# Splitting six seven-fold products a second time in a two-layer fp32 cross-attention kernel

## The chip, the cores and the metric

The kernel runs on one core of a Trainium2 chip. Its time is the device time of one execution in microseconds (us). Three runs before the change took 641.01, 641.02 and 641.52 us; the median is 641.02. Profiled executions are timed too, and their traces are read here.

The core has five engines with queues of their own. TensorE (PE in the profile) multiplies matrices into PSUM; its weight loads are listed apart, as PEld. VectorE (DVE) adds, reduces and transposes 32x32 blocks. ScalarE (ACT) applies functions and copies. GpSimd (POOL) does slow element-wise work and issues transfers. SyncE (SP) issues most transfers. Each engine takes its instructions strictly in order and waits on semaphores for the others.

## The reference

Two layers work on x (8 batches, 100 rows, 1024 columns) and a context c (8 batches, 1444 rows, 512 columns), all in fp32:

```python
# layer 0
Q = x @ Wq + bq; K = c @ Wk + bk; V = c @ Wv + bv
x = x + softmax(Q @ K.T / 32, axis=-1) @ V @ Wo + bo
# layer 1
q = x @ Wq + bq; k = c @ Wk + bk; v = c @ Wv + bv
w = softmax(q @ k.T / 32, axis=1)          # over the 100 rows of x
y = w @ v + x
out = (y - mean(y)) / sqrt(var(y) + 1e-6) * gamma + beta
```

## The kernel before

The kernel never forms K or V. It multiplies weights first: `wqk0` = Wq Wk^T (1024 x 512) and `wvo` = Wv Wo (512 x 1024) for layer 0, and `wqk1` for layer 1. The `queries` are x times wqk (transposed, 512 x 800), and scores are queries times the raw context. What the biases bq, bk and bv contribute are weighted sums over rows of the weights. `accumulate` (L305) forms them on VectorE with one `tensor_scalar` and seven `scalar_tensor_tensor`. `block_sums` (L355) transposes and reduces such a row, and `totals` (L363) finishes it with a small matmul.

**Stages.** In order: qk0 (`weight_products`, L241), vo0 (the same function), queries of layer 0 (L416), qk1, then softmax rounds for layer 0. In round b, `alternated` (L824) weaves the weighted rows of batch b with the scores of batch b+2 on TensorE. Then come `project0` for layer 0's output (L643), queries of layer 1, the rounds and projections of layer 1, and the normalised output.

**Seven-fold products.** Each weight product and each queries stage splits its matrices into 2 x 2 blocks (A11 to A22, B11 to B22) and forms the result from seven block products instead of eight, with sums S1, S2 and so on of the A blocks and T1, T2 and so on of the B blocks. The sums are made by `combine` (L165) on VectorE, often in place over a block that is no longer needed. A block product is `half_product` (L151). It is a run of matmuls over four chunks of 128 rows, accumulated into a pair of PSUM banks. The profile names the banks: qk_x, qk_z, qk_y, qk_w for the weight products of layers 0 and 1, vo_x and so on for vo0, g_x and so on for the queries. `put` copies a finished bank pair to the result with ScalarE, and `add` adds one on VectorE. x and y each hold several products in turn. There are six banks of one pool for x, z and y and two of another for w.

A first-level product in qk0 and qk1 is 16 matmuls of 256 columns, in vo0 eight of 512, in a queries stage eight of 400.

**Buffers.** The weights and the context stream through ten buffers (`unit`), loaded by SyncE (L252 to L267, L499, L510). A load waits until the last reader of its buffer is done. Other pools are small: `row` has 3 buffers, `wide` 2, `gT` 3, and `weight_rows` (the transposed softmax rows) 3. The three `prob` tiles hold scores.

**Order.** TensorE runs in the order of the program. The other engines are ordered by the Tile framework's planner, from the dependencies and from its own estimates of durations, except where the code pins an instruction. `keep_in_program_order` pins it behind the instruction that was traced just before it on its engine. `vector.in_order` (L89) does so for all VectorE instructions issued through `vector`.

Of the kernel before, what the change touches and what calls it, by code (L numbers as in the profile page):

```python
# [25 lines left out]
F32 = mybir.dt.float32  # L26
AF = mybir.ActivationFunctionType
ALU = mybir.AluOpType
# [3 lines left out]
P = 128  # L32
# [23 lines left out]
def two_layer_cross_attention(ctx: ExitStack, tc: tile.TileContext, a: dict, out: bass.AP):  # L56
# [77 lines left out]
    for t in prob:  # L134
        nc.gpsimd.memset(t[T // QD * QD :, :], 0.0)
        nc.gpsimd.memset(t[:, S:], 0.0)
# [14 lines left out]
    def half_product(banks, lhs, rhs, fresh, nb, width):  # L151

        per = nb // len(banks)
        for i in range(len(lhs)):
            for n in range(nb):
                nc.tensor.matmul(  # L156
                    banks[n // per][:, n % per * width : (n % per + 1) * width],
                    lhs[i][:, n * P : (n + 1) * P],
                    rhs[i],
                    start=(fresh and i == 0 and n % per == 0),  # L160
                    stop=(i == len(lhs) - 1),
                    skip_group_check=True,
                )

# [74 lines left out]


    def weight_products(name, left, right, l_width, r_width, scaled):  # L241
# [10 lines left out]
        if name == "qk0":  # L252
            for part in (slice(0, lh // 2), slice(lh // 2, lh)):
                nc.scalar.dma_start(out=units[0][:, part], in_=lsrc[:, 0, part])
            nc.sync.dma_start(out=units[0][:, l_width : l_width + rh], in_=rsrc[:, 0, :rh])
            for h in range(1, EC):
                nc.sync.dma_start(out=units[h][:, :lh], in_=lsrc[:, h, :lh])
                nc.sync.dma_start(out=units[h][:, l_width : l_width + r_width], in_=rsrc[:, h, :])
                if h == 1:
                    nc.sync.dma_start(out=units[0][:, l_width + rh : l_width + r_width], in_=rsrc[:, 0, rh:])  # L260
            for i in range(H):
                for h in (i, H + i):
                    nc.sync.dma_start(out=units[h][:, lh:l_width], in_=lsrc[:, h, lh:])
        else:
            for h in range(EC):
                nc.sync.dma_start(out=units[h][:, :l_width], in_=lsrc[:, h, :])
                nc.sync.dma_start(out=units[h][:, l_width : l_width + r_width], in_=rsrc[:, h, :])  # L267

# [29 lines left out]
        def add(r, c, banks):  # L298
            for j in range(2):
                to = block(r, c, j)  # L300
                nc.vector.tensor_tensor(to, to, banks[j].rearrange("p (n w) -> p n w", n=per), ALU.add)

        accs = {}

        def accumulate(side):  # L305
            for v, of in scaled:
                if of != side:
                    continue
                width = (l_width, r_width)[side]
                if width == E:  # L310
                    acc = row(f"{name}_{v}")
                else:
                    acc = work.tile([P, L], F32, tag="half", name=f"{name}_{v}", bufs=1)
                accs[v] = acc
                for h in range(EC):
                    src = units[h][:, :l_width] if side == 0 else units[h][:, l_width : l_width + r_width]
                    if h == 0:
                        nc.vector.tensor_scalar(acc, src, cols[v][:, h : h + 1], None, ALU.mult)
                    else:
                        nc.vector.scalar_tensor_tensor(acc, src, cols[v][:, h : h + 1], acc, ALU.mult, ALU.add)  # L320
# [5 lines left out]
        combine(S1, A21, A22, ALU.add)  # L326
        Z = pair("z")
        product(Z, A12, B21, True)
        accumulate(1)
        add(0, 0, Z)  # L330
# [3 lines left out]
        combine(B11, B22, T1, ALU.subtract)  # L334
        T2 = B11
        combine(B21, B21, T2, ALU.subtract)
        W = pair("w")
        product(W, A22, B21, True)
        put(1, 0, W)
        combine(S1, S1, A11, ALU.subtract)  # L340
        S2 = S1
        combine(B12, B22, B12, ALU.subtract)
        product(X, S2, T2, False)
        put(0, 1, X)
        accumulate(0)
        combine(A21, A11, A21, ALU.subtract)
        combine(A12, A12, S2, ALU.subtract)
        product(X, A21, B12, False)
        add(1, 0, X)
        add(1, 1, X)  # L350
        product(Y, A12, B22, False)
        add(0, 1, Y)
        return dst, [accs[v] for v, _ in scaled]

    def block_sums(name, t, sums):  # L355

        nc.vector.transpose(t, t)  # L360
        nc.vector.tensor_reduce(sums, t.rearrange("p (c q i) -> p c q i", q=P // QD, i=QD), AX.X, ALU.add)
# [42 lines left out]
    def key_biases(name, kb, bqbk):  # L404

        sums = quarter_sums(name)[:, :B, :]
        t = row(f"{name}_t").rearrange("p (b q j) -> p b q j", q=P // QD, j=QD)
        for g in range(B // G):

            src = bass.AP(kb[g].tensor, kb[g].offset, [list(kb[g].ap[0]), [T, G], [QD, P // QD], [1, QD]])  # L410
            nc.vector.transpose(t[:, g * G : (g + 1) * G], src)
        nc.vector.tensor_reduce(sums, t, AX.X, ALU.add)
        c = totals(name, sums, B)
        nc.vector.tensor_scalar(c, c, SCALE, bqbk, ALU.mult, ALU.add)
        return c

    def queries(layer, w, u):

        H = EC // 2

        def half(g):
            return xT[:, :, g * GT : (g + 1) * GT]

        cols = [slice(j * 256, j * 256 + 256) for j in range(2)]
        A11, A12, A21, A22 = ([w[:, k * H + i, c] for i in range(H)] for c in cols for k in range(2))
        Bs = [[half(g)[:, k * H + i, :] for i in range(H)] for g in range(2) for k in range(2)]
        S1, S2 = (chunks(row(f"g{layer}_s{n}").rearrange("p (c l) -> p c l", c=H), H) for n in (1, 2))
        T1, T2 = (chunks(wide(f"g{layer}_t{n}"), H) for n in (1, 2))
        T3 = chunks(work.tile([P, LC, GT], F32, tag="gT", name=f"g{layer}_t3", bufs=3), H)
        dst = [work.tile([P, LC, GT], F32, tag="gT", name=f"g{layer}T_{g}", bufs=3) for g in range(2)]  # L430
        A, S, T_ = (A11, A12, A21, A22), (S1, S2, A21, A12), (T1, T2, T3, T1)
# [6 lines left out]
        def add(r, g, banks):  # L438
            for j in range(2):
                to = dst[g][:, 2 * r + j, :]  # L440
                nc.vector.tensor_tensor(to, to, banks[j][:, :GT], ALU.add)

        steps = seven_products(
            f"g{layer}",
            A,
            Bs,
            S,
            T_,
            2,
            GT,  # L450
            put,
            add,
            lambda n: left_sums(A, S, (n,)),
            lambda n: right_sums(Bs, T_, (n,)),
        )
        return dst, steps


    wqk0, (acc_c, acc_u) = weight_products(
# [3 lines left out]
    for g in range(B // G):  # L463
# [5 lines left out]
    wvo, (acc_o,) = weight_products("vo0", "L0_xattn_WvT", "L0_xattn_Wo", L, E, (("L0_xattn_bv", 1),))  # L469
    sums_u = quarter_sums("u0")[:, :LC, :]  # L470
    block_sums("u0", acc_u, sums_u)
    sums_c = quarter_sums("c0")
    block_sums("wqbk0", acc_c, sums_c[:, :EC, :])
    gT = [None, None]
    gT[0], steps = queries(0, wqk0, totals("u0", sums_u, LC))
    run(steps)
    block_sums("bvo", acc_o, sums_c[:, EC:, :])
    got = totals("wqbk0", sums_c, 2 * EC)
    wqbk0 = got[:, :EC]
    nc.vector.tensor_tensor(out_bias, out_bias, got[:, EC:], ALU.add)  # L480
    kb0 = [key_bias_sums(f"kb0_{g}", g * GT, (g + 1) * GT, wqbk0) for g in range(B // G)]
    wqk1, (acc_c, acc_u) = weight_products(
        "qk1", "L1_xattn_WqT", "L1_xattn_WkT", E, L, (("L1_xattn_bk", 0), ("L1_xattn_bq", 1))
    )
    c0 = key_biases("c0", kb0, bqbk0)
    for e in range(EC):
        nc.gpsimd.tensor_scalar(xT[:, e, :], xT[:, e, :], out_bias[:, e : e + 1], None, ALU.add)  # L487
    sums = quarter_sums("k1")
    block_sums("u1", acc_u, sums[:, :LC, :])
    block_sums("wqbk1", acc_c, sums[:, LC : LC + EC, :])  # L490
    got = totals("k1", sums[:, : LC + EC, :], LC + EC)
    u1, wqbk1 = got[:, :LC], got[:, LC:]
# [349 lines left out]
    for b in range(B):  # L842
        if b == B - 1:

            o0 = list(project0(AS, A0))
            next(o0[0])
            next(o0[0])
        run(alternated(b, 0, softmax0, A0[b // G][:, :, b % G * T : (b % G + 1) * T]))
        if b == 1:
            AS = value_sums(wvo)  # L850
    next(o0[1])
# [4 lines left out]
    for n in range(6):  # L856
        next(steps)
        if n == 0:
            kb1 = [key_bias_sums(f"kb1_{g}", g * GT, (g + 1) * GT, wqbk1) for g in range(B // G)]
    key_bias[1] = key_biases("c1", kb1, bqbk1)  # L860
# [59 lines left out]
```

## Time and profile before

| what | value |
|---|---|
| median of three runs | 641.02 us |
| profiled execution, its own time | 642.15 us |
| its span, first to last instruction | 640.3 us |
| TensorE busy | 628.8 us (98%) |
| VectorE busy | 457.0 us (71%) |
| ScalarE busy | 132.1 us (21%) |
| GpSimd busy | 101.8 us (16%) |
| moved by transfers | 127.28 MB |

Part 2 of the page divides the span into 40 slices of 16 us, and each digit is the busy share in tenths. The chain that ended last goes back from the last instruction to whatever released it. A line of it reads: start, duration in us, engine, what it writes, line of the program, count. The list of waits reads: who waited for whom, total us, times, longest. TensorE's ends are modelled, since matmuls overlap. The starts of consecutive instructions tell its pace. The same holds for VectorE, where an instruction's duration overlaps a little with the next.

### The profile page before, as it was taken

The numbers are of one execution on the slowest core, as the hardware profiler recorded it, in microseconds if no ns is written. First come the engines' busy times: TensorE is split into PE (matmuls) and PEld (weight loads), VectorE is DVE, ScalarE is ACT, GpSimd is POOL, SyncE is SP. The second block draws the span as 40 slices with busy tenths as digits, with TensorE's granted clock in tenths as the row PEclk, the third lists the DMA queues.
The fourth block names the chain that finished last, engine by engine and source line by source line (L and its number), as shares of the span: only waits on it lengthen the run. The fifth ranks groups of instructions, "written<-read, shape, count | busy, mean of one in ns | idle before, by whom it ended". The sixth has DMA issues, their size and how long they took to land.

```text
span 640.3 us, 9944 instructions
## 1 busy us (share of the span) xinstructions
PE 628.8 (98%) x3968; PEld 518.0 (81%) x3968; DVE 457.0 (71%) x864; ACT 132.1 (21%) x337; POOL 101.8 (16%) x118
## 2 busy tenths in 40 slices
PE   8999999999999999999999999999999999999994
PEld 7886445568885999999998655556999999999992
DVE  5999959569823775666655798229786659898886
ACT  1010010100103333212330000123332340325301
POOL 5000000009200000000010000007212220454054
PEclk9999999999999999999999999999999999999998
DMA  9928019000079799899896303046788990599002
GB/s 290 384 86 333 0 49 340 0 1 0 2 268 364 264 320 302 306 314 323 300 336 214 126 1 131 2 156 212 265 308 306 310 321 35 193 329 333 28 20 83
DMA packets 47907, 127.28 MB, mean 199 GB/s; under 512 B 3890, under 2 KB 6450, under 8 KB 47862
## 3 DMA queue, kind: packets, MB, share of 16 engines
q1 hardware_dynamic: 45784, 120.85, 54.6%
q0 software_dynamic: 1680, 5.33, 2.4%
q8 instruction: 31, 0.51, 0.3%
q10 hardware_dynamic: 398, 0.47, 0.2%
q14 instruction: 14, 0.11, 0.1%
HBM read 123.36 MB, written 3.28 MB: 198 GB/s over the span
## 4 chain that ended last, share of the span: by engine, by line
PE 94%; DVE 2%; issue 1%; DMA 1%; POOL 1%; POOLq 0%; SPq 0%; ACT 0%; DVEq 0%
PE s L560 25%; PE A L531 24%; PE qk_x L156 5%; PE g_x L156 5%; PE o_x L156 5%; PE qk_y L156 4%; PE g_y L156 3%; PE vo_x L156 3%; PE o_y L156 3%; PE qk_w L156 2%; PE vo_y L156 2%; PE g_w L156 2%; PE g_z L156 2%; PE o_w L156 2%; PE o_z L156 2%; PE qk_z L156 1%
## 5 line engine op out<-in xcount | busy, mean ns | idle before, releaser
L531 PE MATMUL A<-w,c 120*128 120x100 f32 (+1 forms) x1536 | 247.5, 265 | 0.0
L531 PEld LDWEIGHTS A<-w,c 120*128 120x128 f32 (+1 forms) x1536 | 215.9, 190 | 0.8
L93 DVE STREAM_TRANSPOSE w<-prob 32x384 f32<-32x384 f32 (+1 forms) x256 | 143.7, 561 | 37.3 <-ACT prob L572 15.1
L560 PE MATMUL s<-cT,g1T 128*100 128x131 f32 (+2 forms) x592 | 122.8, 297 | 0.0
L560 PE MATMUL s<-cT,g0T 128*100 128x131 f32 (+2 forms) x592 | 122.7, 296 | 0.0
L560 PEld LDWEIGHTS s<-cT,g1T 128*100 128x100 f32 x592 | 78.3, 167 | 8.9 <-ACT g1T L436 0.9
L560 PEld LDWEIGHTS s<-cT,g0T 128*100 128x100 f32 x592 | 78.3, 167 | 8.3
L572 ACT ACTIVATE prob<-s,c 100x393 f32<-100x393 f32 (+2 forms) x64 | 35.1, 560 | 116.7 <-PE s L560 116.4
L682 ACT ACTIVATE w<-w,negmax 120x100 f32<-120x100 f32 (+1 forms) x96 | 34.8, 364 | 82.3 <-DVE negmax L93 82.3
L487 POOL TENSOR_SCALAR xT<-xT,L_xattn_bo 128x800 f32<-128x800 f32 x8 | 20.8, 2609 | 134.0 <-PE qk_x L156 134.0
L592 DVE TENSOR_REDUCE maxima<-prob 100x1 f32<-100x394 f32 (+3 forms) x32 | 16.6, 528 | 28.1 <-ACT prob L572 27.9
L156 PE MATMUL qk_x<-qk 128*128 128x256 f32 x128 | 29.0, 382 | 1.0 <-DMA qk<-in_L_xattn_WkT 1.0
L701 POOL TENSOR_TENSOR part<-w 120x500 f32<-120x500 f32 x8 | 10.9, 1365 | 112.9 <-DVE rstd L776 28.6
L156 PEld LDWEIGHTS qk_x<-qk 128*128 128x128 f32 x128 | 23.7, 190 | 5.3 <-DMA qk<-in_L_xattn_WqT 1.3
L865 POOL DMA_DIRECT2D vectors<-in_L_xattn_gamma x1 | 0.6, 604 | 163.2 <-DMA c<-in_ctx 163.2
L320 DVE SCALAR_TENSOR_TENSOR qk_L_xattn_bk<-qk,L_xattn_bk,qk_L_xattn_bk 128x1024 f32<-128x1024 f32 x14 | 17.9, 1277 | 3.3 <-DMA qk<-in_L_xattn_WqT 3.2
L436 ACT ACTIVATE g1T<-g_x,k 128x400 f32<-128x400 f32 x6 | 3.6, 594 | 74.2 <-PE g_x L156 63.8
L93 DVE TENSOR_TENSOR xT<-xT,o_x 128x400 f32<-128x400 f32 (+1 forms) x32 | 15.9, 540 | 3.9 <-PE o_x L156 3.7
L682 ACT ACTIVATION_READ_ACCUMULATOR w<-w,negmax 120x1 f32 (+1 forms) x96 | 17.9, 187 | 0.0
L781 POOL TENSOR_TENSOR z<-z,vectors 100x1024 f32<-100x1024 f32 x7 | 16.5, 2352 | 8.2 <-ACT z L780 8.2
L759 PE MATMUL z<-ident,xT 128*100 128x128 f32 x64 | 16.3, 273 | 0.0
L93 DVE TENSOR_TENSOR w<-w,rtotal 120x400 f32<-120x400 f32 (+1 forms) x24 | 15.6, 649 | 0.7
(212 smaller groups left out, 869.4 us busy)
## 6 DMA issues: line engine op xcount, KB each, us to landing
cT<-in_ctxT SPq DMA_DIRECT2D x64, 722.0 KB, 6.6
c<-in_ctx SPq DMA_DIRECT2D x48, 768.0 KB, 8.5
c<-in_ctx SPq DMA_DIRECT2D x16, 512.0 KB, 6.8
vo<-in_L_xattn_Wo SPq DMA_DIRECT2D x8, 512.0 KB, 5.4
qk<-in_L_xattn_WqT SPq DMA_DIRECT2D x8, 512.0 KB
qk<-in_L_xattn_WqT SPq DMA_DIRECT2D x15, 256.0 KB, 5.4
qk<-in_L_xattn_WkT SPq DMA_DIRECT2D x15, 256.0 KB, 6.3
c<-in_ctx SPq DMA_DIRECT2D x16, 224.0 KB, 6.5
```

Of the source, the lines that this page charges most:

```text
L93: ins = getattr(nc.vector, op)(*args, **kw)
L156: nc.tensor.matmul(banks[n // per][:, n % per * width : (n % per + 1) * width], lhs[i][:, n * P : (n + 1) * P], rhs[i], start=(fresh and i ...
L320: nc.vector.scalar_tensor_tensor(acc, src, cols[v][:, h : h + 1], acc, ALU.mult, ALU.add)
L487: nc.gpsimd.tensor_scalar(xT[:, e, :], xT[:, e, :], out_bias[:, e : e + 1], None, ALU.add)
L531: nc.tensor.matmul(ps[:, k * T : (k + 1) * T], c[m // CQ][:r, m % CQ, k * P : (k + 1) * P], w[:r, m, :], start=(m == 0 and k == 0), stop=( ...
L560: nc.tensor.matmul(banks[n // per][:T, cuts[n] - o : cuts[n + 1] - o], q[:, k, t0 : t0 + T], cT[k][:, cuts[n] : cuts[n + 1]], start=(k == ...
L572: nc.scalar.activation(p[:, part], ps[:T, : part.stop - part.start], AF.Identity, bias=key_bias[layer][:T, b : b + 1], scale=SCALE,)
L592: nc.vector.tensor_reduce(maxima[:, n : n + 1], p[:, part], AX.X, ALU.max)
L682: nc.scalar.activation(w[:r, m0 + m, :], w[:r, m0 + m, :], AF.Exp, bias=negmax[:r, m : m + 1], accum_out=total[:r, m : m + 1])
L701: add(part, w[:MR, 0:5, :], w[:MR, 5:10, :], ALU.add)
L759: nc.tensor.transpose(ps[:T, e * P : (e + 1) * P], xT[:, 4 * j + e, b * T : (b + 1) * T], ident)
L781: nc.gpsimd.tensor_tensor(z, z, beta[:T], ALU.add)
```

## The change

Six of the first-level products are themselves formed from seven half-size products. They are w and the last one of vo0, the same two of qk1, and w of each of the two queries stages. The new function is `inner_product`. It makes four sums when it is called and the other four between its products. Its seven products of w are woven with the matmuls of the product v (A21 by B12, into x's banks). The last product of vo0 and qk1 becomes the inner product `Q`, run on its own after v; its parts are added to the result one by one.

From the third first-level product on, VectorE's instructions of vo0, qk1 and the queries are pinned in the order of the program. The queries' sums are one wide instruction each instead of four.

In qk0 the second product's successor is now w instead of y, with new buffers t2 and t4 for its sums, and its loads come in another order: the left and right first halves, then the right second halves, then the left second halves.

The bias sums of full width in vo0 and qk1 are made by `transferred_sum`. ScalarE scales eight rows into eight buffers (2 `row`, 3 `weight_rows`, 3 `prob`), and transfers issued by GpSimd, which add to their destination, sum them in three levels. qk1's narrow bias sum moves ahead of its products, into the queries stage. Block sums, key-bias sums, the addition of the output bias to x (now on ScalarE, two chunks a round in rounds 0 to 3), the memsets of `prob`'s last rows and layer 0's `value_sums` move to other places.

```diff
     for t in prob:
-        nc.gpsimd.memset(t[T // QD * QD :, :], 0.0)
         nc.gpsimd.memset(t[:, S:], 0.0)
...
+    def inner_product(name, lhs, rhs, nb, width, t, put, add):
+        h, w = nb // 2, width // 2
...
+        combine(S1, A21, A22, ALU.add)
+        combine(T1, B12, B11, ALU.subtract)
+        combine(A21, A11, A21, ALU.subtract)
+        combine(B12, B22, B12, ALU.subtract)
...
+        def steps():
+            X = bank(f"{name}_x")
+            product(X, A11, B11, True)
+            put(0, 0, X)
+            combine(B11, B22, T1, ALU.subtract)
+            combine(A11, S1, A11, ALU.subtract)
+            yield
+            Z = bank2(f"{name}_z")
+            product(Z, A12, B21, True)
+            add(0, 0, Z)
+            combine(B21, B21, B11, ALU.subtract)
+            combine(A12, A12, A11, ALU.subtract)
+            yield
+            Y = bank(f"{name}_y")
+            product(Y, S1, T1, True)
+            put(1, 1, Y)
+            yield
+            product(X, A11, B11, False)
+            put(0, 1, X)
+            yield
+            W = bank2(f"{name}_w")
+            product(W, A22, B21, True)
+            put(1, 0, W)
+            yield
+            product(Y, A12, B22, False)
+            add(0, 1, Y)
+            yield
+            product(X, A21, B12, False)
+            add(1, 1, X)
+            add(1, 0, X)
+            yield
...
@@ weight_products, the loads @@
             for h in range(1, EC):
                 nc.sync.dma_start(out=units[h][:, :lh], in_=lsrc[:, h, :lh])
-                nc.sync.dma_start(out=units[h][:, l_width : l_width + r_width], in_=rsrc[:, h, :])
-                if h == 1:
-                    nc.sync.dma_start(out=units[0][:, l_width + rh : l_width + r_width], in_=rsrc[:, 0, rh:])
+                nc.sync.dma_start(out=units[h][:, l_width : l_width + rh], in_=rsrc[:, h, :rh])
             for i in range(H):
                 for h in (i, H + i):
-                    nc.sync.dma_start(out=units[h][:, lh:l_width], in_=lsrc[:, h, lh:])
+                    nc.sync.dma_start(out=units[h][:, l_width + rh : l_width + r_width], in_=rsrc[:, h, rh:])
+            for h in [H + i for i in range(H)] + list(range(H)):
+                nc.sync.dma_start(out=units[h][:, lh:l_width], in_=lsrc[:, h, lh:])
...
@@ weight_products, the products @@
+        if name == "qk0":
+            t2, t4 = (weight_rows(f"{name}_t{n}") for n in (2, 4))
...
+            W = pair("w")
+            product(W, A22, T4, True)
+            put(1, 0, W)
+        else:
+            combine(S1, A21, A22, ALU.add)
+            Z = pair("z")
+            product(Z, A12, B21, True)
+            if not early:
+                accumulate(1)
+            accumulate(0)
         Y = pair("y")
         product(Y, S1, T1, True)
         put(1, 1, Y)
...
+        if name != "qk0":
+            vector.in_order = True
+            T2, T4 = B11, B21
+            combine(T2, B22, T1, ALU.subtract)
+            add(0, 0, Z)
         combine(S1, S1, A11, ALU.subtract)
         S2 = S1
+        if name != "qk0":
+            combine(T4, B21, T2, ALU.subtract)
         combine(B12, B22, B12, ALU.subtract)
         product(X, S2, T2, False)
         put(0, 1, X)
...
+            V = half_steps(X, A21, B12, False, nb, rh)
...
+            for n, _ in enumerate(inner_product(f"{name}_w", A22, T4, nb, rh, t[:, :768], *parts(1, 0))):
+                run(islice(V, 2 * nb // 4))
+                if n == 2:
+                    combine(A12, A12, S2, ALU.subtract)
+                    add(0, 1, Y)
+                elif n == 3:
+                    _, more = parts(0, 1)
+                    Q = inner_product(f"{name}_q", A12, B22, nb, rh, t[:, 768:1536], more, more)
+                    if between:
+                        between()
+            run(V)
+            add(1, 0, X)
+            add(1, 1, X)
+            run(Q)
+            vector.in_order = False
...
+    def transferred_sum(name, srcs):
+        tiles = [row(f"{name}_{n}") for n in range(2)] + [weight_rows(f"{name}_{n}")[:, :E] for n in range(2, 5)]
+        tiles += [t[:, :E] for t in prob]
+        for t, (src, by) in zip(tiles, srcs):
+            tc.keep_in_program_order(nc.scalar.activation(t, src, AF.Copy, scale=by))
+        n = 1
+        while n < EC:
+            for i in range(0, EC, 2 * n):
+                nc.gpsimd.dma_start(out=tiles[i], in_=tiles[i + n], accum_op=ALU.add)
+            n *= 2
+        return tiles[0]
...
@@ queries @@
+            t = unit(f"g{layer}_w_t")
+            V = half_steps(X, A21, T3, False, nb, GT)
+            for _ in inner_product(f"g{layer}_w", A22, T1, nb, GT, t, *parts(1, 0)):
+                next(V)
+            run(V)
...
@@ two_layer_cross_attention @@
+    run(islice(steps, 2))
+    next(qk1)
+    next(qk1)
+    run(islice(steps, 3))
+    block_sums("bvo", acc_o, sums_c[:, EC:, :], late=True)
     run(steps)
...
+    for t in prob:
+        tc.keep_in_program_order(nc.gpsimd.memset(t[T // QD * QD :, :], 0.0))
...
-    for e in range(EC):
-        nc.gpsimd.tensor_scalar(xT[:, e, :], xT[:, e, :], out_bias[:, e : e + 1], None, ALU.add)
+    def add_out_bias(e):
+        bias = out_bias[:, e : e + 1]
+        tc.keep_in_program_order(nc.scalar.activation(xT[:, e, :], xT[:, e, :], AF.Identity, bias=bias))
...
         run(alternated(b, 0, softmax0, A0[b // G][:, :, b % G * T : (b % G + 1) * T]))
+        for e in range(2 * b, 2 * b + 2) if 2 * b < EC else ():
+            add_out_bias(e)
+        if b == 0:
+            sums = quarter_sums("k1")
+            block_sums("u1", acc_u, sums[:, :LC, :], late=True)
+            block_sums("wqbk1", acc_c, sums[:, LC : LC + EC, :], late=True)
         if b == 1:
+            got = totals("k1", sums[:, : LC + EC, :], LC + EC)
+            u1, wqbk1 = got[:, :LC], got[:, LC:]
+            vector.in_order = True
             AS = value_sums(wvo)
+            vector.in_order = False
```

## The prediction

> **What bounds the kernel now.** I read the page's parts 1 and 2, then the chain that ended last, then TensorE's waits, then the timeline of VectorE for the price of one sum.
>
> ```profile
> span 640.3 us, 9944 instructions
> PE 628.8 (98%) x3968; PEld 518.0 (81%) x3968; DVE 457.0 (71%) x864; ACT 132.1 (21%) x337; POOL 101.8 (16%) x118
> ...
> DVE  5999959569823775666655798229786659898886
> ```
>
> TensorE (PE) is busy 98% of the span, but VectorE (DVE) is nearly full in slices 2 to 7 (16 to 112 us), where the split products lie.
>
> ```profile
> 20.13 0.70 DVE qk_s L93
> 20.82 0.04 issue
> 20.87 7.17 PE qk_y L156 x32
> ...
> 55.87 6.97 PE vo_x L156 x16
> ...
> 97.26 6.87 PE vo_y L156 x16
> 104.25 5.47 PE g_x L156 x16
> ...
> 136.59 5.37 PE g_y L156 x16
> 142.13 6.96 PE qk_x L156 x32
> ...
> 183.71 6.91 PE qk_y L156 x32
> 190.75 0.24 PE k L366 x2
> ```
>
> The chain (start, us, what) shows each first-level product as one piece: 6.91 us in qk0 and qk1, 6.87 in vo0, 5.37 in the queries. From 20.87 us on they join without a gap, until softmax takes over. So PE's own work is the time here, and before 20.87 us it is PE plus these waits:
>
> ```profile
> PE qk_y L156 <- DVE qk_s L93: 1.0, 1, 1.0
> PE qk_x L156 <- DMA qk<-in_L_xattn_WkT: 1.0, 1, 1.0
> ```
>
> qk0's first two products need 2 x 6.91 = 13.8 us and began at 4.43; they could end at 18.3, and the third begins at 20.87: 2.5 us lost.
>
> Prices, from the timelines (start, us, engine, what, count):
>
> ```profile
> 38.26 2.49 DVE L93 TENSOR_TENSOR qk<-qk,qk_s 128x512 f32<-128x512 f32 x4
> 364.01 1.43 DVE L93 TENSOR_TENSOR g_s<-qk 128x256 f32<-128x256 f32 x4
> 525.17 0.64 DVE L93 TENSOR_TENSOR o_t<-A1T,o_t 128x200 f32<-128x200 f32 x2
> 544.13 0.27 PE L759 MATMUL z<-ident,xT 128*100 128x128 f32 x1
> 544.24 0.36 PE L531 MATMUL A<-w,c 120*128 120x100 f32 x2
> ```
>
> Consecutive sums start (2.49 - 0.68)/3 = 0.60 us apart at 512 columns, 0.335 at 256, 0.28 at 200; one lasts 0.08 longer. Each fp32 matmul is two PE instructions: 0.43 us each at 512 columns (6.87/16), 0.216 at 256 (6.91/32), 0.336 at 400, 0.169 at 200 (2.71/16). At 128 columns the next starts 0.11 us later, so halving 256 gains slightly less than half.
>
> [...]
>
> **The change part by part.**
>
> *qk0.* Only left and first right halves go ahead: 8 x 384 KB instead of 512. The trace moved about 0.33 MB/us from 2 us on and a transfer was usable some 1.7 us after its bytes. Step 3 of the first product then has its 1.57 MB by about 9.2 us, when PE gets there at 9.6. The new third product (w) needs right halves (4.2 MB, about 16.7 us) and left second halves of units 4 to 7 (first one about 17.5); VectorE's 12 T sums cost 4 us, mostly before. So w starts near 18.3: -2.5 us. The cover is thin: without it 0 is saved. Loading behind it (xT, vo0) keeps its order.
>
> *vo0.* Removed: 8 bias sums (0.75 + 7 x 1.28 = 9.7 us of VectorE). Added: two second-level products of 14 matmuls x 2 x 0.216 = 6.05 us instead of 6.87, each with 16 narrow sums (8 x 0.20 + 8 x 0.335 = 4.3 us) and 4 or 8 more adds of 256. I count from vo0's first matmul. The third product ends at 20.6, and S2's last sum, in place over S1, waits for it. Everything behind is in fixed order: S2 0.3, T4 2.4, T3 2.4, A21 1.35, first inner sums 2.15 makes 29.3. Then inner sums 2.15, A12 1.35, adds of Y 1.2, first sums of the second inner product 2.15, two block sums 3.55 (the measured 0.6, 0.6, 1.16, 1.16 put between), inner adds 1.35, outer adds 2.4: VectorE is free at 43.5. PE runs x to 27.5 and w woven with v (6.05 + 6.87) to 40.4. The last inner product's three first parts (2.6 us) need none of that. Its fourth needs an add, T2 and S2 behind 43.5: about 44.9, where PE stands ready at 43.0. With some 0.3 us of later waits it ends at 48.6. Before: 104.13 - 55.87 = 48.3. So +0.4, not the -1.6 of the matmuls.
>
> *Queries 0 and 1.* One product each: 28 x 0.169 = 4.74 instead of 5.37, -0.63 each. VectorE's sums are one wide instruction each (1.19 us at 1024 columns, 1.74 at 1600). qk1's 8 short bias sums (5 us) now stand ahead of the add of z; they wait for qk1's last loads, some 6.5 us after vo0 ends, and behind them stand that add, A21, T3 and the last T sum. VectorE then ends its first inner sums 21.1 us after the queries begin, PE needs them at 21.5: hidden by 0.4 us, by more for those needed later. In layer 1, S1 stands behind the 16 key-bias sums (the last at 391.6 before), S1 and T1 take 2.9 us, and the third product starts at 398.4: hidden.
>
> *qk1.* The same sum with the widths exchanged: 56 x 0.11 = 6.16 instead of 6.91; VectorE ends at 43.4, PE's woven part at 40.7, the last product at 48.6, against 48.5: +0.1.
>
> *Bias sums by ScalarE and transfers.* 8 activations x 1.06 us behind x's copy, done about 16 us after a stage starts; in-place sums behind them start at 21. Seven transfers in three levels. Their price I bound [...]by the nearest row, the 400 KB output from GpSimd's queue (7.5 us to landing); I take 7.5 a level. vo0's end near 92 us and are read after 130. qk1's ScalarE part ends near 155; two levels and the moved memsets (3.9 us) end at 174, and ScalarE writes prob near 197: hidden by 22 us. Their issues (7 x 0.6 us a sum, as for the output) block GpSimd's queue until each level has landed; behind them stand only key-bias memsets and, for qk1, prob's. vo0's block sums wait in VectorE's queue for the last level, ahead of the queries' last add and the key-bias sums; late, they would hold up PE's totals. ScalarE's activations stand ahead of y's copy, 4 us early.
>
> *Moved into the score rounds.* xT's bias, off GpSimd (8 x 2.6 us) onto ScalarE, two of about 0.95 us a round (a round is 19.6 us, ScalarE busy under 6). Two block sums (3.55 us) and 32 value sums x 0.335 = 10.7 us on VectorE, which has some 7 us free a round. Split around batch 3's transposes they delay batch 4's maxima by 4 us, its transposes end near 287, and its rows are used at 289: hidden by 2 us, a us of PE for each us beyond.
>
> Sum: -2.5 + 0.4 - 0.6 + 0.1 - 0.6 = -3.2 us. The profiled execution's span 640.3 becomes 637.1, its own time 642.15 becomes 639.0; the median of the runs, 1.1 below that execution, becomes 637.8.
>
> **The rivals.**
>
> *VectorE does not hold the last inner products* (its sums are ready earlier, or wait less): PE takes its 14 matmuls at full pace, another 2.1 + 1.7 us: 634.0. For it: the block sums between could come earlier. Against: the order is fixed in the program.
>
> *The start keeps its wait*: the order of VectorE there is the planner's, and the trace's chain has VectorE pieces and "issue" from 7.84 to 20.82. Then 640.3, no measurable change.
>
> *Slower: VectorE's fixed chain is longer than counted.* In vo0 and qk1 every us more on the 59 VectorE instructions between the third product's end and the last product's fourth part delays the end by one us. If none overlaps the one before (0.08 us each, 59 x 0.08 = 4.7 us a stage), that is +9.4: 647.2. It turns the gain into a loss of more than 0.2% from 2.2 us a stage. Against: dependent sums at 14.37 and 14.70 us in the trace start 0.33 apart.
>
> *The transfers are late.* 155 + 2 L + 3.9 passes 197 when a level L takes over 19 us; at 22 us, +6: 644. Against: 2.5 times the nearest row.
>
> **How the numbers follow.** Forecast (636.3 to 639.5) 0.50; full pace 0.08; start unchanged or half a us lost here and there (639.5 to 642) 0.19; VectorE longer 0.14; transfers or the moved sums late 0.09. The range 634.5 to 644.0 holds the forecast, most of the second, the third and the mild end of the fourth: about 0.8. A change of 0.2% (1.3 us) is about what measurement can tell from none: faster below 639.7: 0.57; same 0.21; slower 0.22.
>
> **What would show it.** qk_w as third product of the chain at 18 to 19 us; vo0 from about 53 to 102; PE waits naming a VectorE sum or add in the last inner products of vo0 and qk1, some 2 us each; queries of about 37 us without a wait; the first scores near 188, free of GpSimd's memsets. Wrong if PE waits inside the woven parts, if ScalarE's prob waits for GpSimd, or if PE's gap near 289 exceeds 1 us.

## The result and the profile after

The changed kernel takes 640.18 us (median of 20 runs, 639.31 to 640.76), the kernel before 641.51 us (20 runs beside them, 640.69 to 642.37). The ratio is 0.9979, with a 95% interval of 0.9972 to 0.9986: 1.33 us faster, where 3.2 us were forecast. A second set of runs gave 640.12 against 641.35. In the profiled execution the span fell from 640.3 to 638.2 us.

Parts 1 and 2 of the page of after, then its list of TensorE's waits:

```profile
span 638.2 us, 10286 instructions
...
PE 625.4 (98%) x4064; PEld 527.6 (83%) x4064; DVE 467.0 (73%) x912; ACT 157.2 (25%) x369; POOL 92.9 (15%) x124
...
DVE  2993699976883797766655579539786659898886
```

```profile
PE vo_q_x L160 <- DVE vo L93: 2.0, 1, 2.0
PE qk_q_x L160 <- DVE qk L93: 1.1, 1, 1.1
PE warm L105 <- DVE ones L102: 1.1, 1, 1.1
PE s L786 <- DVE g1T L93: 0.3, 1, 0.3
```

TensorE's busy time is 3.4 us shorter, its two waits of 1.0 us in the start are gone (the second trace of before, below, has neither), and it has three waits that it did not have. The first two stand where the forecast put them. The third was not forecast. The chain that ended last (start, duration, what) of after:

```profile
4.84 7.33 PE qk_x L160 x32
12.17 6.91 PE qk_z L160 x32
19.08 6.91 PE qk_w L160 x32
...
67.65 6.88 PE vo_y L160 x16
74.91 6.23 DVE vo L93 x12
81.14 1.07 DVE vo_t L93 x4
...
95.71 2.27 DVE vo L93 x5
98.17 0.64 DVE vo L93 x2
98.84 1.13 PE vo_q_x L160 x4
...
102.91 5.47 PE g_x L160 x16
...
170.58 5.10 DVE qk L93 x11
...
184.81 1.16 PE qk_q_x L160 x8
```

From 74.9 to 98.8 us, and again in qk1 from 170.6 to 184.8, the chain runs along VectorE's fixed order, not along TensorE. That is the new limit of those two stages. In vo0 it begins at the last sum of S2, which waits for the third product; in qk1 at the add of the inner product's z, for which VectorE waits 0.62 us.

**Where the time went.** From the timelines of TensorE I took the distance between the first matmuls of successive stages, in two traces of each kernel (us; the last row ends with TensorE's last matmul):

| stretch | before | before, second | after | after, second |
|---|---|---|---|---|
| first two products of qk0 | 16.44 | 15.07 | 14.28 | 14.62 |
| rest of qk0 | 34.86 | 34.76 | 34.76 | 34.76 |
| vo0 | 48.37 | 48.37 | 49.08 | 50.62 |
| queries 0 | 37.87 | 37.87 | 37.23 | 37.23 |
| qk1 | 48.86 | 48.86 | 48.93 | 48.92 |
| rounds of layer 0 | 148.31 | 148.31 | 148.55 | 148.55 |
| project0 | 48.36 | 48.36 | 48.36 | 48.36 |
| queries 1 to the first scores | 32.38 | 32.38 | 31.74 | 31.74 |
| first scores of layer 1 | 9.98 | 9.98 | 10.37 | 10.37 |
| all that follows | 201.93 | 201.93 | 201.95 | 201.95 |

Later stages repeat to 0.02 us, vo0 of the second trace excepted (last section). From vo0 on, the differences of the first traces add up to +0.15 us: the queries' 1.28 us are given back by vo0 (0.71), the first scores (0.39), the rounds (0.24) and qk1 (0.07). Behind TensorE's last matmul the spans differ by some 0.2 us or less. So the gain comes from the first two products of qk0, and those differ from execution to execution.

### The profile page after: what moved, and what is told of

The parts are those of the page before. It is cut to its first block, busy times and chain, and to the rows that moved or that the text cites. A ratio compares the mean times of both kernels' runs of the same rounds, so it can differ in the third digit from the quotient of the medians.

```text
span 638.2 us, 10286 instructions
## 1 busy us (share of the span) xinstructions
PE 625.4 (98%) x4064; PEld 527.6 (83%) x4064; DVE 467.0 (73%) x912; ACT 157.2 (25%) x369; POOL 92.9 (15%) x124
## 4 chain that ended last, share of the span: by engine, by line
PE 91%; DVE 6%; issue 1%; POOL 1%; POOLq 0%; ACT 0%; DVEq 0%
PE s L786 25%; PE A L757 24%; PE qk_x L160 6%; PE g_x L160 5%; PE o_x L160 5%; PE g_y L160 3%; PE qk_y L160 3%; PE o_y L160 3%; DVE vo L93 3%; PE qk_z L160 2%; PE g_z L160 2%; PE o_w L160 2%; PE o_z L160 2%; DVE qk L93 2%; PE vo_x L160 1%
## 5 line engine op out<-in xcount | busy, mean ns | idle before, releaser
L1006 ACT ACTIVATE z<-z,rstd 100x1024 f32<-100x1024 f32 x7 | 8.0, 1150 | 31.9 <-POOL rstd L1003 31.9
L989 DVE SCALAR_TENSOR_TENSOR z<-vectors,r,z 100x512 f32<-100x512 f32 x16 | 11.8, 741 | 4.9 <-PE z L985 4.8
```

The costliest lines, as they stand in the source:

```text
L989: nc.vector.scalar_tensor_tensor(z[:, half], bv1[j][:T], s["r"], ps[:T, :], ALU.mult, ALU.add)
L1006: nc.scalar.activation(z, z, AF.Copy, scale=rstd)
```

## The experiments

Every edit is made on the changed kernel, and its time is compared with 640.1 to 640.2 us. The kernel before, timed beside each set, took between 641.2 and 641.75 us, and most sets have only five executions of an edit. Where a stage's length in the trace can be given, it is the sharper measure.

**What TensorE waits for in vo0 and qk1.** Theory A is the prediction's: the length of VectorE's chain. Theory B: four outer adds that cannot start before the woven part ends. First the block sums and key-bias sums, moved to where VectorE idles:

```diff
             T2, T4 = B11, B21
+            if between:
+                between()
             combine(T2, B22, T1, ALU.subtract)
...
-                    if between:
-                        between()
             run(V)
```

> The block sums (vo0, 3.8 us of VectorE) and the key-bias sums (qk1, 2.45 us) move from the middle of VectorE's fixed order to the stretch where it idles, ahead of the T2 sums (4.75 us idle in vo0, about 2 us and then four times 1 us in qk1). Theory A, the length of VectorE's chain paces the last inner product (the prediction's way of counting): the chain is 3.8 and 2.45 us shorter, so the two waits of TensorE, 2.0 and 1.1 us, vanish: 3.1 us faster than the changed kernel (640.2), so 637.1. Theory B, the four outer adds behind the woven products pace it: they can't start before TensorE ends the woven part (94.3 and 181.1 us in the trace of after), and with 2.5 us for them, 0.3 for the inner add and 1.1 for T2 and S2 the last product's fourth part starts at 98.5 instead of 98.84 in vo0 and at 184.8 as now in qk1: 0.3 us faster, 639.9.

Measured: 637.40 us (637.23 to 638.19), 2.8 us faster. Its list of TensorE's waits has these two:

```profile
PE vo_q_x L160 <- DVE vo L93: 0.6, 1, 0.6
PE qk_q_x L160 <- DVE qk L93: 0.4, 1, 0.4
```

A is nearer: the waits lost 1.4 and 0.8 us, but not all. (The two stages are 1.36 and 0.77 us shorter in the trace; of the rest, its start was 0.4 us shorter than in the first trace of after.) VectorE became 3.8 us shorter in vo0 and the wait only 1.4, because the rest is B. B's own figure was too small, since the first outer add needs only the first of x's two banks, which is done before the woven part ends (the first add starts at 93.06, TensorE ends x at about 93.7). Next the outer adds alone, and then both moves:

```diff
             run(V)
+            run(islice(Q, 2))
             add(1, 0, X)
             add(1, 1, X)
```

> Only the four outer adds (2.5 us of VectorE in vo0 and qk1) move, behind the first two steps of the last inner product; the block sums stay in the middle. Theory B (outer adds): the wait of 2.0 us in vo0 falls to 0.2 and that of 1.1 in qk1 to 0 to 0.2, with small waits in later parts: 2.5 to 3.2 us faster than the changed kernel, so 637.0 to 637.7. If instead the latency inside the last inner product (each part's add and two sums before the next) is what TensorE waits for, both waits stay above 1 us and the time stays at 640.

> Block sums early and outer adds late together. Theory B: as with the outer adds alone, and the last 0.2 us of wait in each stage goes too: 3.0 to 3.6 us faster than the changed kernel, 636.6 to 637.2. Theory A: no more than with the block sums early, 637.1, since TensorE has no wait left.

Measured: 643.96 us (641.61 to 644.93) and 644.11 us (643.90 to 644.99), 3.8 and 3.9 us slower. Both theories failed. The timeline of TensorE, then of VectorE, with both moves (start, us, then the idle time before it in brackets):

```profile
97.08 1.03 PE L160 MATMUL vo_q_x<-vo 128*128 128x256 f32 x4
97.95 1.03 PE L160 MATMUL vo_q_w<-vo 128*128 128x256 f32 x4
101.24 1.49 PE L160 MATMUL vo_q_y<-vo 128*128 128x256 f32 x4 [2.27 <-DVE vo L93]
102.52 1.91 PE L160 MATMUL vo_q_x<-vo 128*128 128x256 f32 x4
```

```profile
98.38 2.48 DVE L93 TENSOR_TENSOR vo<-vo,vo_x 128x512 f32<-128x512 f32 x4
100.77 0.41 DVE L93 TENSOR_TENSOR vo<-vo,vo_q_y 128x256 f32<-128x256 f32 x1
```

The fourth part no longer waits, as B said. The sixth does: it accumulates into y's bank, whose earlier value VectorE reads only behind the outer adds, at 100.77. The wait moved by two parts and grew, from 2.0 to 2.3 us, and in qk1 from 1.1 to 2.1. That is 1.3 us of the 3.9. Most of the loss is something else: behind each of the two waits TensorE ran for some 3.4 us at half its clock (the last part above took 1.91 us instead of 1.03, and with the outer adds alone the granted clock was 0.50 from 102 to 104 us), which costs up to 1.7 us each time; the last section comes back to it. The adds belong behind the fifth step, when all three banks have been read. The same edit with `islice(Q, 5)`, and the block sums early:

> Block sums early as in the first experiment, and the outer adds behind the fifth step of the last inner product (its three reads of y, x and w stand ahead of them now, so that no later part waits for a bank). Theory (the order of VectorE's queue is all that TensorE waits for here): the rest of the two waits, 0.6 and 0.4 us, and the small gaps of 0.1 us a part behind them go: 1.2 us faster than with the block sums early alone (637.4), 636.2, no wait of TensorE in vo0 and qk1. Rival (each part of an inner product is too short for VectorE's add and two sums between parts): waits of 0.3 us or more stay in parts four to six, and the time stays at 637.

Measured: 636.06 us (635.81 to 636.22), 0.9920 of before (0.9907 to 0.9934). The whole list of its waits:

```profile
PE warm L105 <- DVE ones L102: 1.1, 1, 1.1
PE s L787 <- DVE g1T L93: 0.3, 1, 0.3
```

Both waits are gone, vo0 takes 46.78 us and qk1 47.24, together 4.0 us less than in after. Order alone is worth 4.1 us, three times what the change itself gained, and the result beats both kernels.

**What the splits are worth.** `Q` replaced by the whole product, and then neither of the two split:

```diff
-                    Q = inner_product(f"{name}_q", A12, B22, nb, rh, t[:, 768:1536], more, more)
...
-            run(Q)
+            product(Y, A12, B22, False)
+            add(0, 1, Y)
```

> The last first-level product of vo0 and qk1 is computed whole (16 and 32 matmul of TensorE instead of 28 and 56 narrower ones) and VectorE has 24 instructions less a stage. TensorE's last product took 8.5 us in vo0 and 8.0 in qk1 with its waits; whole it takes 6.9 without any. Both theories: 1.6 and 1.1 us less, 637.5. If the waits have another cause than that product (something that the next stage needs), less than 1 us is gained.

> The changed kernel with both split products of vo0 and of qk1 computed whole (VectorE's order, the transfers, the start and the queries as changed). Theory: TensorE has 0.82 us more in vo0 and 0.75 in qk1 for the first of the two; the second took 8.5 and 8.0 us with its waits and takes 6.9: together 1.5 us less than the changed kernel, 638.7. The rival (the splits gain something on the whole): slower than 640.2, at most 643 if every wait is there without them too.

Measured: 637.07 us (636.71 to 637.38) and 639.23 us (638.51 to 639.56). The split of the last product cost 3.1 us (2.65 by the lengths of the two stages), and both splits together cost 0.95 us (1.18 by the stages; my 1.5 was an arithmetic slip: 1.6 + 1.1 less 0.82 and 0.75 is 1.1). With the last product whole, TensorE has no wait in vo0 and qk1, so a better order of VectorE could not shorten them. Since the reordered kernel, with the split, is 1.0 us below that (1.34 by the stages), the split is good and its place in VectorE's queue was bad. The queries' split undone in both layers:

```diff
-            for _ in inner_product(f"g{layer}_w", A22, T1, nb, GT, t, *parts(1, 0)):
-                next(V)
+            W = [bank2(f"g{layer}_w{j}") for j in range(2)]
+            product(W, A22, T1, True)
+            put(1, 0, W)
             run(V)
```

> The changed kernel with the fifth product of the queries, in both layers, computed whole (16 matmuls of 400 columns instead of 28 of 200). Theory: TensorE has 0.63 us more in each layer, and layer 1 loses the wait of 0.34 us at its first scores: +0.9 us, 641.1. Rival: that wait is older than the split (it comes from the four outer adds and stays): +1.3 us, 641.5.

Measured: 641.77 us (641.13 to 642.35), 1.6 us slower. In its trace the two stages are 0.64 us longer each, and the wait at the first scores is still there (0.4 us). The rival holds: the wait is not the split's. Nor is VectorE late for other work: in this trace it idles 12.56 us before the adds in question. In the kernel before, ScalarE copied x's banks to one block of the result and VectorE added them to another, with two adds. Now w is put first and VectorE adds x to both blocks. Its timeline in after:

```profile
416.95 2.21 DVE L93 TENSOR_TENSOR g1T<-g1T,g_x 128x400 f32<-128x400 f32 x4
```

The first matmul of the scores goes ahead and the second waits until 418.73, about the end of the third of these adds. So the likely cause is four adds in a row on VectorE where two had stood; no run puts the old adds and copies back. I tried to cover it with two matmuls of the next product, on top of the best version:

```diff
+            V = half_steps(Y, A12, B22, False, nb, GT)
+            run(islice(V, 2))
             yield
-            product(Y, A12, B22, False)
+            run(V)
```

> As in the experiment with the outer adds after the reads (636.1), and two of the last queries product's sixteen matmuls go ahead of the first scores of layer 1. Theory (the second scores matmul waits for a bank that the third of four adds of the fixed order frees, 0.34 us): those 0.67 us of TensorE cover the wait, 0.3 us faster: 635.7, no wait of TensorE but the one for the first constants. Rival (the wait is for the key biases or the loads): the wait moves behind the two matmuls and the time stays at 636.1.

Measured: 636.22 us (635.96 to 637.09), no gain. The wait is gone, and another has come. (The two matmuls are four PE instructions and took 1.34 us, not 0.67.) From the list of waits:

```profile
PE A L760 <- ACT w L911: 0.8, 1, 0.8
```

At 438.93 TensorE wants the softmax rows of batch 0, which ScalarE finishes at its own pace. Scores that start later leave less work behind them to cover it. In this form nothing was gained; one matmul ahead, half as much, was not tried.

**What the transfers buy.** The bias sums on VectorE again, in the changed kernel and in the best version:

```diff
-                if width == E and name != "qk0":
+                if False:
                     accs[v] = transferred_sum(f"{name}_{v}", srcs)
```

> The changed kernel with the full-width bias sums of vo0 and qk1 on VectorE again (8 instructions, 9.7 us a stage), without ScalarE's eight activations and the seven adding transfers. Theory (VectorE's order paces the last inner product): VectorE has 6 to 9 us of idle time in each stage ahead of the second inner product's first sums, in pieces of 1 to 5 us, so between 1 and 4 us a stage are pushed onto the end: 642 to 648. Rival (the transfers buy nothing, the sums fit the idle time): 640.2.

> As in the experiment with the outer adds after the reads (636.1), and the full-width bias sums on VectorE again, without ScalarE's activations and the adding transfers. Theory (the bias sums fit VectorE's idle time ahead of the S2 sums, which wait for TensorE until 74.6 us in vo0 and 161 us in qk1): 636.1 again, the transfers buy nothing even where the last products do not wait. Rival (with the block sums moved there too, 9.7 and 3.8 us are more than the idle time holds): VectorE ends the S2 sums later than TensorE needs them, 1 to 3 us slower, and the wait stands at the product of S2 and T2.

Measured: 640.07 us (639.34 to 640.79) and 636.06 us (635.87 to 636.49): the transfers buy nothing in either. VectorE of the first of the two, in vo0:

```profile
59.46 2.60 DVE L93 SCALAR_TENSOR_TENSOR vo_L_xattn_bv<-vo,L_xattn_bv,vo_L_xattn_bv 128x1024 f32<-128x1024 f32 x2
61.97 2.49 DVE L93 TENSOR_TENSOR vo<-vo,vo_s 128x512 f32<-128x512 f32 x4
66.92 0.69 DVE L93 TENSOR_TENSOR vo<-vo,vo_z 128x512 f32<-128x512 f32 x1 [2.46 <-PE vo_z L160]
...
74.57 0.42 DVE L93 TENSOR_TENSOR vo_s<-vo_s,vo 128x256 f32<-128x256 f32 x1 [1.29 <-PE vo_y L160]
```

The 9.7 us end before 62.1, and VectorE then still idles for z and for S2, whose last sum waits for TensorE until 74.57, as in after (74.55). With the transfers, VectorE idled in the same place, 4.75 us, for ScalarE's activations.

**The start.** Loads and products of qk0 as before; then only the loads; then only the products (y third instead of w):

```diff
-                nc.sync.dma_start(out=units[h][:, l_width : l_width + rh], in_=rsrc[:, h, :rh])
+                nc.sync.dma_start(out=units[h][:, l_width : l_width + r_width], in_=rsrc[:, h, :])
+                if h == 1:
+                    nc.sync.dma_start(out=units[0][:, l_width + rh : l_width + r_width], in_=rsrc[:, 0, rh:])
             for i in range(H):
                 for h in (i, H + i):
-                    nc.sync.dma_start(out=units[h][:, l_width + rh : l_width + r_width], in_=rsrc[:, h, rh:])
-            for h in [H + i for i in range(H)] + list(range(H)):
-                nc.sync.dma_start(out=units[h][:, lh:l_width], in_=lsrc[:, h, lh:])
+                    nc.sync.dma_start(out=units[h][:, lh:l_width], in_=lsrc[:, h, lh:])
```

> The changed kernel with the loads and the order of products of before in qk0; all else stays. Theory: the start alone is worth what the two traces show at the first matmul of vo0, 2.06 us: 642.2. Rival: that difference is mostly one execution against another (the first product of the changed kernels took between 6.9 and 7.7 us in five traces): 1.3 us or less, 641.5 or below.

> The changed kernel with the loads of qk0 in the order of before (whole rows of the right matrix, then the left second halves), and the new order of products. Theory (the new order of the loads lets the first product run earlier, and the new third product matters less): most of the 1.7 us that the whole start is worth is lost: 641.3 or above, with a first product of about 8 us and the third at 19.9. Rival (the order of the products is the gain, since w's operands, not y's, come early in either order of loads): 640.5 or below.

> The changed kernel with the loads of qk0 in the new order and the products in the old one (y third, which needs the left second halves that now come last). Theory (the two belong together): y waits for loads that end about 21 us after the start, so the third product begins at 22 to 23 us: 643 to 644. Rival (the loads are never late): the first product as short as in the changed kernel, 640.2.

Measured: 641.91 us (640.96 to 643.47), 641.24 us (640.34 to 643.38) and 646.68 us (644.89 to 647.59). Some executions of the first two, and of the changed kernel, had a mean clock of 0.993 or 0.994, which the last section takes up. Among those at 0.995 and above the medians are 641.56, 641.12 and, for the changed kernel of the second set, 640.06. So the start is worth 1.5 us, of which the loads alone make 1.1. The traces agree: the first two products took 15.07 to 16.44 us in the four traces with the old loads, and 13.82 to 14.79 in the twelve with the new loads and the new order of products. The first product with the old loads waits twice for them. TensorE's timeline with the old loads:

```profile
9.24 1.97 PE L160 MATMUL qk_x<-qk 128*128 128x256 f32 x8 [0.47 <-DMA qk<-in_L_xattn_WkT]
11.63 1.97 PE L160 MATMUL qk_x<-qk 128*128 128x256 f32 x8 [0.42 <-DMA qk<-in_L_xattn_WkT]
```

The old products with the new loads wait 2.8 us for S1, whose second halves now come last, and then run slow (the same view):

```profile
22.18 8.86 PE L160 MATMUL qk_y<-qk_s 128*128 128x256 f32 x32 [2.80 <-DVE qk_s L93]
```

The new order of products is therefore what the new loads need. With the old loads it is worth 0.4 us. Last, both kernels once more:

> The kernel before once more, for a second trace of its start. If the start varies from one execution to the next (as the first product of the changed kernels does, 6.9 to 7.8 us), the third product begins at 19.9 to 20.6 us instead of 20.87, and every later stage has the lengths of the first trace within 0.1 us. Otherwise it begins at 20.8 to 20.9 again and the 0.6 us that this execution had above the median lie elsewhere.

> The changed kernel once more beside the two above, for a second trace of its start. Theory (only qk0's first two products differ from one execution to the next): every later stage as in the first trace within 0.05 us, the third product between 18.6 and 19.7 us, 640.2. Rival: other stages differ by 0.2 us or more.

Measured: 641.09 us for the one execution of before, and 640.12 us (639.20 to 641.90, 22 runs) for after. The start of before in its second trace (the chain):

```profile
12.96 6.91 PE qk_z L156 x32
19.87 6.91 PE qk_y L156 x32
26.77 6.91 PE qk_w L156 x32
```

The third product began at 19.87, not at 20.87. No wait for VectorE stood there: the first product took 8.12 us, waiting in small pieces, and VectorE's sum was ready before the second ended. In after the third began at 19.08 and 19.42. The theory of the last expectation held but for one stage: vo0 took 1.5 us more (last section).

## Why the prediction was right or wrong, step by step

The direction and the place of the two waits were right, but the gain was 1.3 us instead of 3.2. Four terms of the sum were mis-sized: 1.0 us at the start, 0.3 in vo0, 0.2 in qk1 and the rounds, 0.4 behind the queries of layer 1.

- **qk0, "-2.5 us": the largest miss.** The step was "they could end at 18.3, and the third begins at 20.87: 2.5 us lost". Measured by undoing it, it is 1.5 us. One end of the difference was an execution with a late start (19.87 in the other trace). The other end, 18.3, assumed a first product of 6.91 us from 4.43 on. It began at 4.6 in all later traces and, with the new loads, took 6.9 to 7.9 us. The forecast priced the loads of the fourth of the product's four steps and called that cover thin. In both traces of after the time was lost earlier, in the first two steps. In the second trace:

```profile
4.63 2.07 PE L160 MATMUL qk_x<-qk 128*128 128x256 f32 x8
7.09 5.42 PE L160 MATMUL qk_x<-qk 128*128 128x256 f32 x24 [0.38 <-DMA qk<-in_L_xattn_WkT]
```

- **vo0, "+0.4": measured +0.71.** The forecast put the fourth part at 44.9 us of the stage with TensorE ready at 43.0. Counted from vo0's first matmul (53.67 us), TensorE was ready at 43.05, and the part began at 45.2, 0.3 us late. The parts behind it came 0.97 us apart instead of 0.86, which is the 0.3 us "of later waits". What was too small is the start of VectorE's fixed order: S2's last sum, which waits for the third product, began at 20.9 us of the stage (74.55), not at 20.6. The order from there to the end of the outer adds took 22.95 us, as reckoned (22.9). VectorE's timeline in after:

```profile
74.55 0.43 DVE L93 TENSOR_TENSOR vo_s<-vo_s,vo 128x256 f32<-128x256 f32 x1 [1.29 <-PE vo_y L160]
...
97.50 0.42 DVE L93 TENSOR_TENSOR vo<-vo,vo_q_x 128x256 f32<-128x256 f32 x1
```

- **qk1 and the rounds, "+0.1": measured +0.31.** A wait of 1.1 us stands there as in vo0. VectorE was free 43.6 us after the stage's first matmul where the forecast had 43.4; in its fixed order it had idled 0.62 us for the inner product's z, which the count leaves out. A totals matmul moved from qk1 into the rounds, which is why the two are taken together. The rounds themselves were otherwise hidden, as forecast.
- **Queries, "-0.6" twice: right to 0.01 us in both layers (0.63 reckoned, 0.64 measured).** But the forecast ended at the last woven matmul. It did not look at what stands next in TensorE's queue in layer 1, the first scores, and at VectorE's four adds on the banks that they need: +0.39. The undoing of the split cleared the split. That the four adds in a row are the cause is read from the timelines and not shown by an experiment.
- **Bias sums by ScalarE and transfers: hidden, as forecast.** Five of the activations of 1024 columns in vo0 kept ScalarE busy for 5.3 us, 1.06 each, as counted. The levels took 5.2 to 7.2 us from issue to landing in vo0 and 5.7 to 6.6 in qk1, below the 7.5 that the forecast took. In vo0 the transfers read (KB each, median us to landing):

```profile
vo_L_xattn_bv<-vo_L_xattn_bv POOLq DMA_DIRECT2D x4, 512.0 KB, 5.2
vo_L_xattn_bv<-prob POOLq DMA_DIRECT2D x2, 512.0 KB, 5.3
prob<-prob POOLq DMA_DIRECT2D x1, 512.0 KB, 7.2
```

  What the forecast missed is that the work they replace was hidden as well. It counted the 9.7 us as removed from VectorE, and never asked where VectorE idles. The forecast's number did not suffer, since its count begins behind S2.
- **The rival "VectorE does not hold the last inner products"** was priced at 3.8 us more and had "the block sums between could come earlier" in its favour. The order that does it gained 4.1 (2.3 and 1.7 in the two stages, where 2.1 and 1.7 were priced), but needed the outer adds moved too. The slower rival's rule, each us of VectorE one us of the end, was not met when VectorE's order became shorter: in vo0 3.8 us less behind S2's last sum gave 1.4, because the outer adds then waited for TensorE. Ahead of that sum 9.7 us cost nothing.
- **The median.** The forecast took 1.1 us off a profiled execution whose excess over the median lay in the very start that the change edits. It was thus counted twice, in the 2.5 us of qk0 and again in the step to the median; it is the same us as in the first item.

## What to carry to other kernels

In an order fixed by hand, look for the point up to which the engine waits for others: work ahead of it is free as far as it fits that idle time, and work behind it is paid until the other engine becomes the limit. Put deferred adds behind the reads that free a bank for the other engine, not merely behind the operands it needs next; one step too early and the wait only changes its place. And cost a stage that waits for loads from several executions, since one trace of it can be off by more than the change is worth (here 16.44 us in one trace of before and 15.07 in the other, for a gain of 1.33).

## What the runs showed of the hardware

**A wait of 2 us can cost more than itself.** The second trace of after has the same wait of 1.96 us in vo0, but the stage took 50.62 us instead of 49.08. Its windows around it, the granted clock in the column behind POOL:

```profile
core 0: us, PE busy (x) PEld busy (x) DVE busy (x) ACT busy (x) POOL busy (x), PEclk, DMA share, GB/s
...
100.00:101.00 1.00, 1.00 (x5) 0.78 (x4) 1.00 (x5) 0.00 (x0) 0.00 (x0) 0.79 0.02 6
101.00:102.00 1.00, 1.00 (x4) 0.73 (x4) 0.59 (x3) 0.00 (x0) 0.00 (x0) 0.50 0.00 0
...
103.00:104.00 1.00, 1.00 (x4) 0.82 (x3) 0.42 (x1) 0.00 (x0) 0.00 (x0) 0.51 0.03 8
104.00:105.00 1.00, 1.00 (x6) 0.83 (x6) 0.31 (x1) 0.00 (x0) 0.00 (x0) 1.00 0.92 143
```

TensorE resumed at 99.18 us. At about 100.6 its clock fell to 0.50 for some 3.4 us, which cost 1.5 us. In the first trace of after it stayed at 1.00 through the same wait. Mean clocks of 0.993 or 0.994 go with one such fall in the traces. With the wait of 1.96 us unchanged, they stood in none of the first 20 executions of after, 3 of the second 22, 2 of 21 with whole queries, none of 21 with the bias sums on VectorE, but 10 of 21 with the old start and 5 of 14 with the old loads. Why the start matters is open.

Waits of 2.1 to 2.3 us (outer adds late, two a kernel) gave 0.990 or 0.991, two falls, in 7 of 9 executions and 5 of 5 with both moves, and no trace shows one behind a wait of 1.1 us or less. Five traces have eight falls between them. Four of these stand in windows like those above: by the clock lost there, each lasted about 3.4 us and began about 0.1, 0.4, 1.1 or 1.4 us after TensorE resumed.

So the same wait of 1.96 us is followed by a fall in some executions and not in others, and what decides it was not shown. Such falls account for the excess of the old products with the new loads (646.7 where 643 to 644 was expected): their wait of 2.8 us was followed by a clock of 0.50 from about 23.2 us on (1.8 us), and the one of 1.96 us in vo0 by another fall (a part of 1.91 us where after has 1.13).

**Narrow sums.** Two VectorE sums of 128 columns in after took 0.50 us (from 88.21 us on), and the next instruction started 0.40 us after the first: they start 0.20 us apart and last 0.30. The forecast's estimate was 0.20 us apart, which is also what a line through the wider sums of before gives (0.60 us apart at 512 columns, 0.335 at 256).
